# Layer 3: VectorE convolves the four upper rows of image b's strips, TensorE the four lower rows of both halves in joint rounds, and ScalarE copies the halo rows

## The chip, the cores and the metric

The kernel runs on one core of a Trainium2 chip. The metric is the device time of one execution in microseconds; three executions of the kernel before took 14472.04 to 14497.12 us, with a median of 14486.18 us.

## What is computed

A batch of images with 48 channels and 256 x 256 pixels goes through four residual layers, each `x = x + layer(groupnorm(x))`. Layers 1 and 2 are scans along rows and columns. Layer 3, the one that is changed, is cut to this:

```python
y = einsum('oc,bchw->bohw', w_in, x)            # 48 -> 288 channels
f = rfft2(blocks of 8 x 8 of y) * fft_mask      # scaled in the frequency domain
y = irfft2(f)                                   # back to pixels
y = depthwise 3 x 3 convolution of y with w_dw  # zero padding of 1
x1, x2 = split(y, 2, axis=1)                    # 144 channels each
return einsum('oc,bchw->bohw', w_out, gelu(x1) * x2)
```

Layer 0 is built of the same parts (a 1x1 convolution, a depthwise 3 x 3 one, a gated product, an 8 x 8 DFT), in another order and with 96 gated channels.

## The kernel before, in words

Everything is in float32, and a float32 matmul shows as two records in the trace.

`layer3` takes two images, a and b, at a time: two pairs, each cut into 32 strips of RB = 8 rows and a 33rd short step, the tail, which holds the last row of the convolution. That makes 64 full strips and two tails. The convolution's output is one row behind its input, so a strip needs two rows of the strip above it, its halo.

One strip runs through these steps (lines of the profile in brackets):

- `fetch` loads x (SyncE's DMA queue), `normed` applies the group norm on ScalarE and gives the tile `u` (L909).
- `turned` transposes `u` on TensorE into `pt` (L921), and ScalarE copies that to `xt` (L925). `waves` applies the DFT, `pf` (L935), and ScalarE copies it to `xf` (L936).
- `spectrum` multiplies by `w_in` on TensorE, `pz` (L946), and VectorE multiplies the result by the mask into `z` (L948, L952); 16 calls a strip, in eight pieces of two.
- `pixels` turns `z` back into pixels, `pp` (L977), and ScalarE copies them into one of the five tiles `z_a0`, `z_a1`, `z_b0`, `z_b1`, `z_m` (L981). Tile `z_a0` holds the first 128 of the 144 channels of x1 of image a, `z_a1` those of x2; `z_m` holds the remaining 16 channels of both halves and both images. Before that the two halo rows are copied from the tile's own lower end: by ScalarE for `z_m` (L968), by GpSimd for the other four (L970).
- `taps` is the convolution on TensorE (L994): for each of the nine taps, eight matmuls with a diagonal 32 x 32 weight, four pairs of rows by two blocks of 32 channels, summed in the PSUM tile `pd`.
- `gate`: Gelu of x1 on ScalarE, `gl` (L1008), and the product with x2 on VectorE, `g_a`, `g_b` or `g_m` (L1009).
- `mixed` is the product with `w_out` on TensorE, `po` (L1022), 40 matmuls a strip of 32 rows by 64 columns of the array; VectorE adds the residual, `xo` (L1035), and SyncE's queue stores it.

All PSUM tiles come from one pool of four buffers (`ps_w`), each of two banks.

The order of TensorE's work is written by hand (`manual_schedule` for that engine); the other engines' queues are ordered by a scheduler at build time. Two generators `lane(0)` and `lane(1)` give the taps: lane 0 works on channel blocks 0 and 1, lane 1 on blocks 2 and 3, each through a0, a1, gate, b0, b1, gate, and m in every second strip. A third generator, `work`, gives all other pieces. `in_turns` draws them together: in each turn it takes one tap from each lane, a joint round, and then as many pieces as their costs allow, with a credit of `pace` for each lane that moved. Lane 1 starts four rounds later. A piece has a condition, and the pieces come in order: `back` (pixels) waits until both lanes have taken the tile's former strip, `store` (mixed) until all taps of the strip are taken. A lane gates strip n only once strip n - 1 is stored.

Layer 0 has the same machinery with one generator more: `aside` runs "units" on VectorE beside the lanes. A unit convolves a tile with eight `scalar_tensor_tensor` taps for each half of its rows (L313) on an accumulator that ScalarE starts with the first tap (L307). Then follow Gelus on ScalarE (L321, L322). In layer 0 the orders of both TensorE and VectorE are written by hand.

Of the kernel before, what the change touches and what calls it, by code (L numbers as in the profile page):

```python
# [15 lines left out]
C = 48  # L16
# [12 lines left out]
class Net:  # L29
# [782 lines left out]
    def layer3(self, x, scs):  # L812
# [2 lines left out]

        nc, tc, W, H, NQ, HD = self.nc, self.tc, self.W, self.H, self.NQ, HID3
        NM, NR, WP, R2 = 128, HID3 - 128, W + 2, MM // W
        steps = [(p, s) for p in range(self.NP) for s in range(H // RB + 1)]  # L820
        tail = lambda step: step[1] == H // RB
        with ExitStack() as st:
            pool = lambda name, bufs, **k: st.enter_context(tc.tile_pool(name=name, bufs=bufs, **k))
            wp, io, mid = pool("w3", 1), pool("io3", 2), pool("mid3", 1)
            ps_w = pool("ps3w", 4, space=PSUM)
            st.enter_context(tc.manual_schedule(engines={mybir.EngineType.PE}))


            parts = [(0, 0, NM), (HD, NM, NM), (NM, 2 * NM, NR), (HD + NM, 2 * NM + NR, NR)]
# [23 lines left out]
            for k in range(3):  # L853
                for t in range(9):
                    nc.vector.tensor_scalar(diag[:, k, t, :], eye, wd[:, k, t : t + 1], None, ALU.mult)


            wo = wp.tile([128, 6, 64], F32, name="wo")
            nc.gpsimd.memset(wo, 0.0)
            for j in range(4):  # L860
                s = slice(32 * j, 32 * j + 32)
                nc.sync.dma_start(
                    wo[s, 0:4, 0:C], self.a["L3_w_out"][0:NM, :].rearrange("(k c) o -> c k o", c=32)
                )
                for b in range(2):
                    at = 32 * j + NR * b
                    nc.sync.dma_start(wo[at : at + NR, 4 + b, 0:C], self.a["L3_w_out"][NM:HD, :])
# [35 lines left out]

            def normed(step):
                raw, sc = raw_of[step], scp[step[0]]
                u = mid.tile([112, NQ, 2, RB, PW // 2], F32, name="u")
                for e in range(2):
                    for l in range(2):
                        nc.scalar.activation(  # L909
                            u[:, l::2, e].rearrange("p v h w -> p v (h w)"),  # L910
                            raw[0:112, e, :, :, l * 8 : l * 8 + 8].rearrange("p (v f) h w -> p v (f h) w", f=2),
                            AF.Identity, bias=sc[0:112, 1:2], scale=sc[0:112, 0:1],
                        )
                return u
# [13 lines left out]
                return xt  # L928

            def waves(xt):  # L930
                xf = mid.tile([112, NQ, 128], F32, name="xf")
                for q0 in range(0, NQ, 8):
                    pf = ps_w.tile([128, 8, 128], F32, name="pf", tag="w")
                    for q in range(8):
                        nc.tensor.matmul(pf[0:112, q, :], xt[:, q0 + q, :], self.dft_p, start=True, stop=True)  # L935
                    nc.scalar.copy(xf[:, q0 : q0 + 8, :], pf[0:112])  # L936
                return xf
# [23 lines left out]
            def pixels(step, g, k):  # L961

                n, at, old = (64, 64 * (step[1] % 2), 64 - 64 * (step[1] % 2)) if g == "m" else (128, 0, 0)
                t, above = zt[g][at : at + n], zt[g][old : old + n]
                if step[1] == 0:
                    nc.gpsimd.memset(t[:, 0:2, 1 : W + 1], 0.0)
                elif g == "m":
                    nc.scalar.copy(t[:, 0:2, 1 : W + 1], above[:, RB : RB + 2, 1 : W + 1])  # L968
                else:
                    nc.gpsimd.tensor_copy(t[:, 0:2, 1 : W + 1], above[:, RB : RB + 2, 1 : W + 1])  # L970
                if tail(step):
                    nc.gpsimd.memset(t[:, 2, 1 : W + 1], 0.0)
                    return
                for q0 in range(0, NQ, 8):
                    pp = ps_w.tile([128, 2, RB, 4 * PW], F32, name="pp", tag="w")
                    for q in range(8):
                        nc.tensor.matmul(  # L977
                            pp[0:n, q // 4, :, q % 4 * PW : (q % 4 + 1) * PW],
                            z[:, q0 + q, k * NM : k * NM + n], self.idft, start=True, stop=True,
                        )  # L980
                    nc.scalar.copy(  # L981
                        t[:, 2 : RB + 2, 1 + q0 * PW : 1 + (q0 + 8) * PW].rearrange("p h (k w) -> p k h w", k=2),
                        pp[0:n],
                    )
# [3 lines left out]
            def taps(step, g, half, blocks, pd):  # L988
                for t in range(9):
# [8 lines left out]
                            )  # L998
                    yield True

            def gate(step, img, k0, x1, x2):
                n = 32 if tail(step) else 128
                m = W if tail(step) else MM
                flat = lambda ap: ap.rearrange("p k r w -> p k (r w)")[0:n, :, 0:m]
                gl = io.tile([128, 2, MM], F32, name="gl")
                to = gated[img]
                k1 = k0 + (1 if img == "m" else 2)
                nc.scalar.activation(gl[0:n, 0 : k1 - k0, 0:m], flat(x1), AF.Gelu)  # L1008
                nc.vector.tensor_tensor(to[0:n, k0:k1, 0:m], gl[0:n, 0 : k1 - k0, 0:m], flat(x2), ALU.mult)  # L1009

            def mixed(step):

                p, s = step
                h0 = s * RB - 1
                js, n = (range(1), 1) if tail(step) else (range(4), R2)
                pos = [ps_w.tile([128, 2, R2, W], F32, name="po", tag="w") for _ in js[::2]]
                for i in range(5):
                    for j in js:
                        for b in range(2):
                            r = slice(32 * j, 32 * j + 32)  # L1020
                            src = gated["m"][r, 0] if i == 4 else gated["ab"[b]][r, i]
# [29 lines left out]
            def lane(l):  # L1051

                for n, step in enumerate(steps):
                    for img in ("a", "b") + (("m",) if step[1] % 2 == l else ()):
                        pds = []
                        for half in range(1 if img == "m" else 2):
                            g = img if img == "m" else f"{img}{half}"
                            while (step, g) not in ready:
# [8 lines left out]
                        else:  # L1067
                            gate(step, img, 2 * l, *pds)

            def work():  # L1070

                def back(step, k):
# [3 lines left out]
                        pixels(step, order[k], k)  # L1078
                        ready.add((step, order[k]))

                    free = lambda: last not in steps or k == 4 or taken.get((last, order[k]), 0) == 2
                    return free, 0.0 if tail(step) else 3.8, go

                def both(*fs):
                    return lambda: [f() for f in fs]
# [2 lines left out]
                always = lambda: True  # L1088

                def front(step):  # L1090
                    yield always, 1.8, lambda: state.update(xt=turned(state["u"]))
                    yield always, 3.8, lambda: state.update(xf=waves(state["xt"]))

                def spectra():
                    for q in range(0, NQ, 2):
                        yield always, 1.2, both(*[lambda q=q + i: spectrum(state["xf"], q) for i in range(2)])

                def store(step):
                    full = lambda: all(taken.get((step, g), 0) == (1 if g == "m" else 2) for g in order)

                    def go():
                        mixed(step)
                        out.add(step)

                    return full, 4.5, go

                fetch(steps[0])
                state["u"] = normed(steps[0])
# [24 lines left out]
                        yield back(nxt, 1)  # L1133
                yield store(steps[-1])

            self.in_turns([lane(0), lane(1)], work(), 0.6)


@with_exitstack
# [103 lines left out]
```

## Time and profile before

| what | us |
|---|---|
| median of three runs | 14486.18 |
| the profiled execution | 14477.21 |
| its span, first to last instruction | 14475.4 |
| TensorE busy | 13474.0 (93%) |
| VectorE busy | 5981.7 (41%) |
| ScalarE busy | 3295.6 (23%) |
| GpSimd busy | 1496.9 (10%) |
| layer 3, from 9064 us to the end | 5411.4 |

Durations in the profile are those of one execution. "PE" is TensorE, "PEld" its weight loads, "DVE" VectorE, "ACT" ScalarE, "POOL" GpSimd, "SP" SyncE. A group of instructions is shown with its line, engine and operation, then output and inputs with the shape, the count, the busy time in us and the mean of one in ns, and last the engine's idle time before it with what ended that. Matmuls overlap each other, so the mean of one is longer than its share of the time. The chain of waits goes back from the last instruction to what released it each time.

### The profile page before, as it was taken

The page shows a single profiled execution, that of the slowest core. Times are in us where ns is not written, and L with a number is a line of the kernel's source. Part 1 is how long each engine was busy: PE and PEld are TensorE (multiplying, and loading weights), DVE is VectorE, ACT ScalarE, POOL GpSimd, SP SyncE. Part 2 cuts the span into 40 slices and gives each one's busy share as a digit, 9 for nine tenths or more (in the row PEclk, how much of TensorE's full clock was granted, in tenths as well). Part 3 has the DMA queues.
Part 4 walks back from the last instruction along what each step waited for, and adds up shares of the span by engine and source line. Part 5 has one row for each costly group of instructions (what it writes and reads, how often), then busy time and mean ns, then how long its engine had stood idle before and what let it go on. Part 6 is the DMA issues. An engine that isn't in the chain of part 4 may idle for free.

```text
span 14475.4 us, 377862 instructions
## 1 busy us (share of the span) xinstructions
PE 13474.0 (93%) x175216; PEld 8571.1 (59%) x175216; DVE 5981.7 (41%) x10946; ACT 3295.6 (23%) x3108; POOL 1496.9 (10%) x1228
## 2 busy tenths in 40 slices
PE   2999999999998998899989988899999999999999
PEld 1444444446776775667767756566666666666666
DVE  6777777773333344533333445222222222222222
ACT  1333333332232000022320000222222222222222
POOL 0000010000000014400000144000000000000000
PEclk9999999999999998999999988999999999999999
DMA  7222222217756867677577676211111111111110
GB/s 166 53 49 53 54 51 51 54 41 146 145 144 162 152 132 190 160 156 145 145 167 151 135 190 156 31 20 24 21 20 24 20 20 20 24 20 20 24 20 18
DMA packets 1168867, 1221.55 MB, mean 84 GB/s; under 512 B 1025860, under 2 KB 1030460, under 8 KB 1106428
## 3 DMA queue, kind: packets, MB, share of 16 engines
q1 hardware_dynamic: 1069180, 649.60, 23.5%
q0 software_dynamic: 87488, 445.55, 11.0%
q10 hardware_dynamic: 10624, 102.24, 3.5%
q8 instruction: 1375, 22.53, 0.7%
q14 instruction: 200, 1.64, 0.0%
HBM read 699.82 MB, written 497.42 MB: 83 GB/s over the span
## 4 chain that ended last, share of the span: by engine, by line
PE 80%; DVE 8%; DMA 6%; issue 2%; ACT 1%; POOL 1%; SPq 1%; ACTq 0%; DVEq 0%; POOLq 0%
PE acc L598 33%; PE pd L994 20%; PE pp L977 8%; PE pd L278 4%; PE pz L946 4%; DVE acc L313 3%; DMA blk<-x 3%; PE po L1022 2%; PE pf L935 2%; PE ph L249 2%; DMA x<-blk 1%; PE pf L386 1%; DVE xo L419 1%; DMA gx<-in_x 1%; PE py L355 1%
## 5 line engine op out<-in xcount | busy, mean ns | idle before, releaser
L598 PE MATMUL acc<-line,w_down 96*96 96x256 f32 x12240 | 2649.9, 379 | 43.8 <-DMA in<-x 23.3
L598 PEld LDWEIGHTS acc<-line,w_down 96*96 96x96 f32 x12240 | 1995.6, 163 | 697.5 <-issue 44.6
L994 PE MATMUL pd<-z_b,diag 32*32 32x512 f32 x37152 | 1810.9, 596 | 10.5 <-DVE g_a L1009 10.5
L994 PE MATMUL pd<-z_a,diag 32*32 32x512 f32 x37152 | 1794.4, 596 | 0.1
L598 PE MATMUL acc<-line,w_left 96*96 96x256 f32 x6120 | 1360.8, 385 | 246.9 <-DVE line L781 246.9
L598 PE MATMUL acc<-line,w_right 96*96 96x256 f32 x6120 | 1336.9, 381 | 103.0 <-DVE line L742 39.1
L598 PEld LDWEIGHTS acc<-line,w_left 96*96 96x96 f32 x6120 | 1015.9, 166 | 591.5 <-DVE line L781 252.9
L278 PE MATMUL pd<-main,diag 32*32 32x512 f32 x36864 | 1337.7, 601 | 10.5 <-DVE g L292 5.4
L313 DVE SCALAR_TENSOR_TENSOR acc<-rest,wd,acc 128x1024 f32<-128x1024 f32 x1024 | 1313.7, 1324 | 72.5 <-ACT acc L307 70.6
L977 PEld LDWEIGHTS pp<-c_idft,z 128*128 128x128 f32 x10240 | 1156.8, 181 | 287.0 <-issue 265.3
L598 PEld LDWEIGHTS acc<-line,w_right 96*96 96x96 f32 x6120 | 1003.3, 164 | 436.6 <-DVE line L742 40.7
L977 PE MATMUL pp<-c_idft,z 128*128 128x128 f32 x10240 | 1223.8, 278 | 17.6 <-ACT z_b L981 17.6
L994 PEld LDWEIGHTS pd<-z_a,diag 32*32 32x32 f32 x37152 | 697.7, 103 | 508.1 <-issue 318.8
L948 DVE TENSOR_TENSOR z<-pz,mask 128x512 f32<-128x512 f32 x1024 | 701.5, 685 | 698.5 <-PE pz L946 698.5
L278 PEld LDWEIGHTS pd<-main,diag 32*32 32x32 f32 x36864 | 524.3, 103 | 681.6 <-issue 505.4
L994 PEld LDWEIGHTS pd<-z_b,diag 32*32 32x32 f32 x37152 | 619.0, 103 | 455.5 <-issue 278.6
L742 DVE SCALAR_TENSOR_TENSOR line<-acc,b_right,in 96x256 f32<-96x256 f32 x1020 | 489.4, 480 | 882.2 <-PE acc L598 836.8
L661 DVE TENSOR_TENSOR line<-acc,in 96x256 f32<-96x256 f32 x1020 | 429.1, 421 | 928.3 <-PE acc L598 900.2
L701 DVE SCALAR_TENSOR_TENSOR line<-acc,b_down,in 96x256 f32<-96x256 f32 x992 | 476.2, 480 | 808.5 <-PE acc L598 808.5
L791 POOL TENSOR_TENSOR blk<-blk,line 96x1024 f32<-96x1024 f32 x248 | 705.5, 2873 | 861.2 <-DVE line L781 447.4
L102 ACT ACTIVATE nrm<-nrm 96x2 f32<-96x2 f32 (+1 forms) x4 | 0.8, 204 | 3331.1 <-DVE nrm L101 3331.1
L1008 ACT ACTIVATE gl<-pd 128x1024 f32<-128x1024 f32 (+2 forms) x330 | 302.3, 926 | 1970.8 <-PE pd L994 1639.3
(147 smaller groups left out, 12161.3 us busy)
## 6 DMA issues: line engine op xcount, KB each, us to landing
blk<-x ACTq DMA_DIRECT2D x64, 1536.0 KB, 24.0
in<-x SPq DMA_DIRECT2D x248, 384.0 KB, 11.1
dn<-line POOLq DMA_DIRECT2D x124, 768.0 KB, 9.6
rt<-line POOLq DMA_DIRECT2D x124, 768.0 KB, 10.3
in<-rt SPq DMA_DIRECT2D x124, 768.0 KB, 7.3
in<-dn SPq DMA_DIRECT2D x120, 768.0 KB, 7.1
in<-up SPq DMA_DIRECT2D x240, 384.0 KB, 11.1
up<-blk POOLq DMA_DIRECT2D x56, 1536.0 KB, 24.0
```

The lines of the kernel that those rows point to most:

```text
L278: nc.tensor.matmul(pd[32 * j : 32 * j + 32, i], diag[s, t, :], z[s, R2 * j + t // 3 : R2 * j + t // 3 + R2, t % 3 : t % 3 + W], start=(t = ...
L313: nc.vector.scalar_tensor_tensor(to, at(t, r), wd[:, 1, t : t + 1], to, ALU.mult, ALU.add)
L598: self.nc.tensor.matmul(acc, w[:, t, :], carry[:, :, t : t + m], start=(t == 0), stop=(t == 2))
L661: nc.vector.tensor_tensor(blocks(inner(line)), blocks(acc), xin[p][:, :, r % 2, :, r // 2, :], ALU.add)
L701: nc.vector.scalar_tensor_tensor(inner(line), acc, bd, new[p][r], ALU.add, ALU.add)
L742: nc.vector.scalar_tensor_tensor(blocks(inner(line)), blocks(acc), br, new, ALU.add, ALU.add)
L791: (nc.vector if w0 == 0 else nc.gpsimd).tensor_tensor(part, part, inner(ln[p][:, f::2])[..., lo:hi].rearrange("p w i h -> p i h w"), ALU.add)
L946: nc.tensor.matmul(pz[:, b, 0 : 2 * HD], xf[s, q, :], wi[s, :], start=True, stop=True)
L948: nc.vector.tensor_tensor(z[:, q, 0 : 2 * n].rearrange("p (b c) -> p b c", b=2), pz[:, :, 0:n], mask[:, :, 0:n].to_broadcast([128, 2, n]), ...
L977: nc.tensor.matmul(pp[0:n, q // 4, :, q % 4 * PW : (q % 4 + 1) * PW], z[:, q0 + q, k * NM : k * NM + n], self.idft, start=True, stop=True,)
L994: nc.tensor.matmul(pd[32 * j : 32 * j + 32, i, 0:n, :], diag[s, 2 if g == "m" else half, t, :], zt[g][s, R2 * j + t // 3 : R2 * j + t // 3 ...
L1008: nc.scalar.activation(gl[0:n, 0 : k1 - k0, 0:m], flat(x1), AF.Gelu)
```

## The change

All of it is in `layer3`.

- Image b's taps are divided. The four upper rows of a strip's output (row pairs 0 and 1) are convolved on VectorE by `unit`, which `aside` runs: for each half, b0 and b1, ScalarE starts the accumulator with tap 0, VectorE adds taps 1 to 8 over 128 channels by 4 rows by 256 columns. After half 0 ScalarE applies Gelu to it, after half 1 VectorE multiplies the two.
- The four lower rows stay on TensorE in `lower_taps`: in one round a lane takes both halves (x1 to output partitions 0 to 63, x2 to 64 to 127), so image b takes nine rounds of a lane where it took 18. `lower_gate` follows.
- `mixed` takes the upper rows of image b from the accumulator with two matmuls of full depth and a new weight tile `wo_b`, ahead of the others, and leaves out the eight pairs that did this (b = 1, j < 2, i < 4).
- The halo rows of a and b are copied by ScalarE instead of GpSimd.
- VectorE's order in layer 3 is written by hand too. `store` waits for the unit's product as well, `back` for the unit's taps, and the pieces have new costs; `pace` is 0.65 instead of 0.6.
- `u` and `xf` share one buffer.

The diff, cut to its core:

```diff
-            st.enter_context(tc.manual_schedule(engines={mybir.EngineType.PE}))
+            st.enter_context(tc.manual_schedule(engines={mybir.EngineType.PE, mybir.EngineType.DVE}))
+            HR = RB // 2
...
+            wo_b = wp.tile([128, 64], F32, name="wo_b")
+            nc.gpsimd.memset(wo_b, 0.0)
+            nc.sync.dma_start(wo_b[:, 0:C], self.a["L3_w_out"][0:NM, :])
...
-                u = mid.tile([112, NQ, 2, RB, PW // 2], F32, name="u")
+                u = mid.tile([112, NQ, 2, RB, PW // 2], F32, name="u", tag="u")
...
-                xf = mid.tile([112, NQ, 128], F32, name="xf")
+                xf = mid.tile([112, NQ, 128], F32, name="xf", tag="u")
...
-                elif g == "m":
+                else:
                     nc.scalar.copy(t[:, 0:2, 1 : W + 1], above[:, RB : RB + 2, 1 : W + 1])
-                else:
-                    nc.gpsimd.tensor_copy(t[:, 0:2, 1 : W + 1], above[:, RB : RB + 2, 1 : W + 1])
...
+            def lower_taps(step, blocks, pd):
+                for t in range(9):
+                    for half in range(2):
+                        for j in range(2, 4):
+                            to = slice(64 * half + 32 * (j - 2), 64 * half + 32 * (j - 1))
+                            for i, k in enumerate(blocks):
+                                s = slice(32 * k, 32 * k + 32)
+                                nc.tensor.matmul(
+                                    pd[to, i], diag[s, half, t, :],
+                                    zt[f"b{half}"][s, R2 * j + t // 3 : R2 * j + t // 3 + R2, t % 3 : t % 3 + W],
+                                    start=(t == 0), stop=(t == 8),
+                                )
+                    yield True
+
+            def lower_gate(k0, pd):
+                gl = io.tile([128, 2, MM], F32, name="gl")
+                flat = pd.rearrange("p k r w -> p k (r w)")
+                nc.scalar.activation(gl[64:128], flat[0:64], AF.Gelu)
+                nc.vector.tensor_tensor(gated["b"][64:128, k0 : k0 + 2], gl[64:128], flat[64:128], ALU.mult)
...
+            whole, full = {}, set()
+
+            def unit(step, half):
+                g, rows, made = f"b{half}", 1 if tail(step) else HR, []
+                at = lambda t: zt[g][:, t // 3 : t // 3 + rows, t % 3 : t % 3 + W]
+
+                def start():
+                    acc = mid.tile([128, HR, W], F32, name=f"acc{half}", tag=f"acc{half}", bufs=2 - half)
+                    made.append(acc[:, 0:rows])
+                    nc.scalar.activation(made[0], at(0), AF.Identity, bias=none, scale=wd[:, half, 0:1])
+
+                def tap(t):
+                    nc.vector.scalar_tensor_tensor(
+                        made[0], at(t), wd[:, half, t : t + 1], made[0], ALU.mult, ALU.add
+                    )
+                    if t == 8:
+                        taken[step, g] = taken.get((step, g), 0) + 1
+
+                def curve():
+                    nc.scalar.activation(made[0], made[0], AF.Gelu)
+                    whole[step] = made[0]
+
+                def product():
+                    nc.vector.tensor_tensor(whole[step], whole[step], made[0], ALU.mult)
+                    full.add(step)
+
+                taps = [(0.05 + 0.31 * rows, lambda t=t: tap(t)) for t in range(1, 9)]
+                last = [(3, 0.0, curve)] if half == 0 else [(2, 1.28, product)]
+                return lambda: (step, g) in ready, start, taps, last
...
+                part = whole.pop(step)
+                for j in js[:2]:
+                    nc.tensor.matmul(
+                        pos[0][64:128, j, 0:n, :], wo_b, part[:, R2 * j : R2 * j + n, :], start=True, stop=False
+                    )
                 for i in range(5):
                     for j in js:
                         for b in range(2):
+                            if b and j < 2 and i < 4:
+                                continue
...
+                        if img == "b":
+                            while (step, "b0") not in ready or (step, "b1") not in ready:
+                                yield False
+                            if not tail(step):
+                                pds.append(ps_w.tile([128, 2, R2, W], F32, name="pd", tag="w"))
+                                yield from lower_taps(step, (2 * l, 2 * l + 1), pds[0])
+                            for g in ("b0", "b1"):
+                                taken[step, g] = taken.get((step, g), 0) + 1
+                            while n and steps[n - 1] not in out:
+                                yield False
+                            if pds:
+                                lower_gate(2 * l, pds[0])
+                            continue
...
-                        yield always, 1.2, both(*[lambda q=q + i: spectrum(state["xf"], q) for i in range(2)])
+                        yield always, 1.2, both(*[lambda q=q + i: spectrum(state["xf"], q) for i in range(2)]), 2.0
...
-                    return full, 4.5, go
+                    return done, 6.4, go, 3.5
...
-            self.in_turns([lane(0), lane(1)], work(), 0.6)
+            side = self.aside([unit(s, k) for s in steps for k in range(2)])
+            self.in_turns([lane(0), lane(1)], work(), 0.65, side)
```

More of the change, by code (lines that the diff above doesn't have):

```diff
@@ L855, in layer3 @@
                     nc.vector.tensor_scalar(diag[:, k, t, :], eye, wd[:, k, t : t + 1], None, ALU.mult)
+            none = wp.tile([128, 1], F32, name="none")
+            nc.gpsimd.memset(none, 0.0)
             wo = wp.tile([128, 6, 64], F32, name="wo")
             nc.gpsimd.memset(wo, 0.0)
+            wo_b = wp.tile([128, 64], F32, name="wo_b")
+            nc.gpsimd.memset(wo_b, 0.0)
+            nc.sync.dma_start(wo_b[:, 0:C], self.a["L3_w_out"][0:NM, :])
             for j in range(4):
@@ L1068, in lane @@
                             gate(step, img, 2 * l, *pds)
+            units = {g: 3 if g[0] == "b" else 1 if g == "m" else 2 for g in order}
             def work():
@@ L1079, in go @@
                         ready.add((step, order[k]))
-                    free = lambda: last not in steps or k == 4 or taken.get((last, order[k]), 0) == 2
-                    return free, 0.0 if tail(step) else 3.8, go
+                    free = lambda: last not in steps or k == 4 or taken.get((last, order[k]), 0) == units[order[k]]
+                    return free, 0.0 if tail(step) else 3.8, go, 0.0
                 def both(*fs):
@@ L1090, in front @@
                 def front(step):
-                    yield always, 1.8, lambda: state.update(xt=turned(state["u"]))
-                    yield always, 3.8, lambda: state.update(xf=waves(state["xt"]))
+                    yield always, 1.8, lambda: state.update(xt=turned(state["u"])), 0.0
+                    yield always, 3.8, lambda: state.update(xf=waves(state["xt"])), 0.0
                 def spectra():
                     for q in range(0, NQ, 2):
-                        yield always, 1.2, both(*[lambda q=q + i: spectrum(state["xf"], q) for i in range(2)])
+                        yield always, 1.2, both(*[lambda q=q + i: spectrum(state["xf"], q) for i in range(2)]), 2.0
                 def store(step):
-                    full = lambda: all(taken.get((step, g), 0) == (1 if g == "m" else 2) for g in order)
+                    done = lambda: step in full and all(taken.get((step, g), 0) == units[g] for g in order)
                     def go():
```

## The prediction

> **What bounds the kernel now.** I read the busy time by stretches first, for the last layer alone and for two of its strips; then the chain of waits, for the length of a strip.
>
> ```profile
> 9064.00:14475.40 5411.40, 5348.13 (x106162) 3309.34 (x106162) 1329.24 (x2918) 1414.89 (x1547) 174.28 (x294) 1.00 0.12 21
> 12037.98:12205.00 167.02, 165.39 (x3307) 102.40 (x3312) 41.15 (x90) 43.87 (x48) 4.93 (x8) 1.00 0.12 21
> ...
> 11870.95 17.94 PE pd L994 x503
> 12037.98 17.94 PE pd L994 x503
> ```
>
> Columns of the first two: stretch and length, then busy us (instructions) of TensorE, its weight loads, VectorE, ScalarE, GpSimd, then granted clock, DMA share, GB/s. Layer 3 takes 5411 us, TensorE is busy 99% of it at full clock, VectorE 25%, ScalarE 26%. The same place of the chain comes back after 167.03 us, two strips: **83.5 us a strip**, 64 full strips.
>
> Then the groups of layer 3 and (last two) layer 0, and TensorE's waits:
>
> ```profile
> L994 PE MATMUL pd<-z_b,diag 32*32 32x512 f32 x37152 | 1810.9, 596 | 10.5 <-DVE g_a L1009 10.5
> L968 ACT COPY z_m<-z_m 64x512 f32<-64x512 f32 x64 | 39.5, 617 | 2.0
> L925 ACT COPY xt<-pt 128x896 f32<-128x896 f32 x128 | 109.9, 909 | 195.4 <-PE pt L921 195.4
> L307 ACT ACTIVATE acc<-rest,none,wd 128x1024 f32<-128x1024 f32 x122 | 151.6, 1242 | 188.9 <-DVE rest L261 187.2
> L313 DVE SCALAR_TENSOR_TENSOR acc<-rest,wd,acc 128x1024 f32<-128x1024 f32 x985 | 1264.3, 1324 | 72.5 <-ACT acc L307 70.6
> ...
> PE pp L977 <- ACT z_b L981: 17.6, 15, 1.2
> PE pd L994 <- DVE g_a L1009: 10.5, 46, 0.2
> ```
>
> Here TensorE waits for nobody: 28 us in 64 strips. So each microsecond of waiting that the change brings is lost in full, as each microsecond of work it takes away is won.
>
> Layer 0 already splits its convolution between TensorE and VectorE, so its timeline shows what such a split can cost:
>
> ```profile
> 1533.57 1.06 ACT L321 ACTIVATE gr<-acc 64x1024 f32<-64x1024 f32 x1 [0.46 <-DVE acc L313]
> 1534.77 1.06 ACT L322 ACTIVATE gr<-acc 64x1024 f32<-64x1024 f32 x1
> 1535.85 1.04 ACT L323 COPY acc<-acc 64x1024 f32<-64x1024 f32 x1
> 1536.80 1.01 ACT L289 ACTIVATE gl<-pd 128x1024 f32<-128x1024 f32 x1
> 1537.86 1.75 PE L372 MATMUL pt<-c_ident,y 112*128 112x112 f32 x16 [1.58 <-ACT gl L289]
> ```
>
> TensorE stands 1.58 us because the Gelu that frees its PSUM buffer (L289) is queued on ScalarE behind Gelus that waited for VectorE's taps.
>
> [...] a joint round of both lanes (32 records of 0.596 us) comes every 1.06 us. [...]
>
> **The change, part by part** (per full strip).
>
> *Taps leave TensorE.* Counted in both instruction orders, joint rounds fall from 2664 to 2052, 9 a full strip and 36 short ones in the two tails. 9 x 1.06 = **9.5 us less**.
>
> *The output product.* 32 of its 80 records on image b go, 4 of full depth come (2 matmuls, two records each) ahead of the rest. Image a still needs the ten groups that set the 4.47 us of the old product. The four cost 1.98 us in layer 0 (L257, 112 deep, 512 columns, four in 1.98). They use only half the columns, so the last may overlap: bounds 0 and 2.0; I take **1.8 more**.
>
> *VectorE.* 16 taps of 128x1024 and one product. Layer 0's tap takes 1.324 us, but one follows the other every 1.20, since its neighbours work on two halves of a tile. Here each tap reads what the one before wrote. Bounds 1.20 and 1.37 (duration and a handoff); I take 1.32. 16 x 1.32 + 1.2 = 22 us on an engine with 62 us free: its amount costs nothing, its order may.
>
> *ScalarE.* Two starts (1.24), one Gelu (1.06), four halo copies (0.62) taken over from GpSimd, where they waited up to 27 us for taps without harm: 6 us on an engine with 61 free. The wo_b load and the memsets are once: nothing beside the 20 us that the first matmul waits for a weight load anyway; 2 us if not.
>
> *The new waits.* VectorE's queue is now in program order, ScalarE's is the scheduler's. In the changed kernel's order ScalarE has, after each store: Gelu of acc0 (waits for VectorE's 8th tap), Gelu of a0 (frees a PSUM buffer), two pixel copies of z_b1, start of acc1, halo copy of z_b1 (waits for the 5th tap of acc1), then the copies of xt that the next DFT needs. VectorE has the eight xo additions, the acc0 taps left over, and all of acc1. Behind a tap thus queue a PSUM release and a transpose copy that TensorE needs. One strip, from the end of the output product:
>
> VectorE: xo 2.8 (eight took 2.74), 5 taps to 9.4. ScalarE: Gelu 10.5, Gelu of a0 11.5. TensorE: 4 rounds and pp (3.77) done at 8.1, then needs the buffer: **waits 3.4**. ScalarE: two copies (1.03) to 13.5, start to 14.8. VectorE: 5 taps to 21.4. ScalarE: halo 22.0, xt 22.9. TensorE: from 11.5 three rounds, pt (1.7), one round: 17.5, then needs xt: **waits 5.4**. Small waits in the spectra (a pz buffer used again after 0 or 2 matmuls, where VectorE's 0.74 is in between) and for g_m: 0.9. Sum 9.7.
>
> The other three patterns, walked the same way: pair 0 with 4 taps left 4.0 + 4.6 + 1.7 = 10.3; pair 1 with 6 left 5.0 + 4.1 + 1.0 = 10.1; pair 1 with 4 left: product for g_m 3.0, b's taps for a g_a multiply that stands behind 4 taps of acc1 5.4, one pp on a single buffer 1.2, spectra on a single buffer 4.7, together 14.3. Mean **11.1 us more**.
>
> *Sum:* -9.5 + 1.8 + 11.1 = +3.4 us a strip, x 64 = +215. Tails: 36 short rounds gone, one chain of 16 short taps bare at the very end: 10 us either way, taken as 0. The profiled execution took 14477 us (span 14475), 9 under the median; against the median 14486 + 215 = **14700**.
>
> With a tap at 1.20 the walk gives 9.7 of waits, +2.0 a strip, 14615; with 1.37, +4.1, 14750. An error of 1 us in the walk's other terms is 64 us: own range 14550 to 14850.
>
> **Rivals.** *The cover holds* (faster): VectorE and ScalarE run early enough, TensorE waits little. For it: layer 0 has the same design, busier (VectorE 2160 of 2900 us), and its TensorE idles only 220 us in 64 strips, 3.4 each. With 3.4 here: -9.5 + 1.8 + 3.4 = -4.3 x 64: **14210**. Against it: layer 0's tail taps are spread through the strip, here 12 to 14 stand in one block between store and DFT. Place: the waits for pd's release and for xt. It decides below 7.7 us of waits a strip: then faster. *They cancel* (7 to 8 us): **14486**. *The waits are larger*: taps over 1.4 us, or a halo copy that also holds up the pixel copies of image a; at 15 us of waits a strip, +7.3 x 64: **14950**. That VectorE doesn't take over the rows is excluded by the order, which has its 16 taps a strip.
>
> **How the numbers follow.** Forecast 0.70, cover holds 0.15, cancel 0.07, larger 0.08. Within 0.2% (29 us) is about what a measurement of this kernel can tell from no change. Faster by more 0.15, same 0.07, slower 0.78. The range goes from 14470 (takes in most of the cancel case) to 14850 and leaves out 0.15 below and 0.05 above.
>
> **What would show it.** Right: in layer 3 a strip takes 86 to 88 us, TensorE's busy share falls to some 87%, VectorE's rises to 50%; TensorE's longest waits are pf for ScalarE's xt (4 to 6 us, 48 times) and pd or pp for ScalarE's gl (3 to 5 us), ScalarE's are the Gelu of acc0 and the z_b1 halo copy for VectorE's taps; the dependent taps come every 1.32 us. Wrong: a strip under 83 us, or waits on ScalarE under 1 us; then ScalarE's order or the tap's pace was misjudged. If the four full-depth records take over 2.5 us, that term was.

## The result and the profile after

The changed kernel takes **14831.6 us** (median of four executions, 14821.3 to 14836.3) against 14484.2 for the kernel before: ratio 1.0239, 95% interval 1.0221 to 1.0256. The forecast was 14700. Its profiled execution has a span of 14819.5 us, 344.1 more than before. Of e10's four executions below, two took 15497 and 25725 us at a mean granted clock of 0.88 and 0.51, where the other two had 0.97, and are left out.

The busy time by stretches of the changed kernel comes first: all of layer 3, then six stretches of one strip of pair 0 that follow each other. The columns are those of the prediction's first view; the last three are the granted clock (the share of its full clock that TensorE was given), DMA share and GB/s.

```profile
9064.00:14819.50 5755.50, 5178.42 (x86662) 3005.19 (x86662) 2734.59 (x4036) 1775.43 (x1997) 15.73 (x30) 0.95 0.10 20
10020.01:10023.42 3.41, 1.02 (x22) 0.83 (x29) 1.26 (x1) 2.12 (x3) 0.00 (x0) 1.00 0.36 35
10023.42:10026.83 3.41, 3.41 (x65) 1.29 (x66) 0.41 (x1) 3.38 (x4) 0.00 (x0) 0.50 0.02 5
10026.83:10030.25 3.42, 3.42 (x80) 2.28 (x79) 3.35 (x3) 0.07 (x1) 0.00 (x0) 1.00 0.00 0
10030.25:10033.66 3.41, 0.84 (x32) 0.00 (x0) 3.30 (x4) 0.58 (x2) 0.00 (x0) 1.00 0.02 5
10033.66:10037.07 3.41, 2.51 (x12) 2.51 (x13) 3.30 (x4) 2.58 (x4) 0.00 (x0) 0.50 0.00 0
10037.07:10040.49 3.42, 3.42 (x18) 3.42 (x18) 1.14 (x1) 1.01 (x1) 0.00 (x0) 0.50 0.00 0
```

The whole 344 us lie in layer 3 (5755.5 against 5411.4). TensorE is busy 90% of it and idle 577 us, where it was idle 63. But its busy time fell by 170 us only, 2.7 a strip, where the prediction took 7.7 away. The granted clock tells why: it was 1.00 throughout layer 3 before, and is 0.95 now. It isn't 0.95 evenly. TensorE stands still from 10020.94 to 10023.33 and from 10031.09 to 10034.56, and after each of these waits it works at **half the clock** (0.50) for some microseconds.

The clock records of the traces show when. In layer 3 every change of the clock lies on a grid of 3.413 us, the stretches of the view above (all 225 changes from 9110 us on in the changed kernel, to 5 ns). In the changed kernel half clock lasts one stretch of the grid 67 times out of 113, two 40 times and three 4 times. Ahead of a fall stands a stretch in which TensorE was little busy: 1.02 and 0.84 of 3.41 us ahead of the two falls here. Counted over the twelve traces of this case, from 9110 us on, all 430 stretches at full clock in which TensorE was busy less than 0.40 of the time were followed by half clock, 152 of 326 from 0.40 to 0.62, and 2 of 17309 above that; in the changed kernel alone it was 90 of 90, 22 of 55 and 1 of 2932. Full clock never came back after a stretch that was busy less than 0.80; in the changed kernel the 112 stretches ahead of a return were busy at least 0.83.

The timeline of the same strip, ScalarE, VectorE and TensorE:

```profile
10017.40 0.62 ACT L975 COPY z_b<-z_b 128x512 f32<-128x512 f32 x1 [12.25 <-DVE acc L1053]
10021.31 1.06 ACT L1060 ACTIVATE acc<-acc 128x1024 f32<-128x1024 f32 x1 [3.29 <-DVE acc L1053]
10022.27 1.01 ACT L1035 ACTIVATE gl<-pd 128x1024 f32<-128x1024 f32 x1
10025.15 1.24 ACT L1050 ACTIVATE acc<-z_b,none,wd 128x1024 f32<-128x1024 f32 x1
10033.08 0.62 ACT L975 COPY z_b<-z_b 128x512 f32<-128x512 f32 x1 [6.18 <-DVE acc L1053]
10033.61 1.71 ACT L932 COPY xt<-pt 128x896 f32<-128x896 f32 x2
...
10014.71 6.56 DVE L1053 SCALAR_TENSOR_TENSOR acc<-z_b,wd,acc 128x1024 f32<-128x1024 f32 x5
10026.42 10.53 DVE L1053 SCALAR_TENSOR_TENSOR acc<-z_b,wd,acc 128x1024 f32<-128x1024 f32 x8 [5.15 <-ACT acc L1050]
...
10017.10 3.84 PE L982 MATMUL pp<-c_idft,z 128*128 128x128 f32 x32
10023.33 5.01 PE L999 MATMUL pd<-z_a,diag 32*32 32x512 f32 x96 [2.39 <-ACT gl L1035]
10028.26 1.75 PE L928 MATMUL pt<-c_ident,u 112*128 112x112 f32 x16
10034.56 6.63 PE L942 MATMUL pf<-c_dft_p,xt 128*112 128x128 f32 x32 [3.47 <-ACT xt L932]
10041.11 3.41 PE L999 MATMUL pd<-z_a,diag 32*32 32x512 f32 x96
```

The chain is the one that the prediction forecast: VectorE's last acc0 tap ends at 10021.3, the Gelu of acc0 has waited for it (L1060), the Gelu of a0 that frees TensorE's buffer stands behind that. Then the halo copy of z_b1 (L975) waits 6.18 us for the fifth tap of acc1, and the copies of xt stand behind that. What was not forecast are two durations on TensorE. The 96 records (three joint rounds) after the first wait take 5.01 us, at full clock 3.41 (last line); pf takes 6.63 us, at full clock 3.75. Taps come every 1.31 us (10.53 for eight).

TensorE's longest waits in the changed kernel, and the two of ScalarE that cause them (total us, times, longest):

```profile
PE pf L942 <- ACT xt L932: 139.7, 42, 5.1
PE pd L999 <- ACT gl L1035: 104.1, 31, 8.1
PE pd L1015 <- DVE g_a L1036: 64.3, 15, 4.4
PE pp L982 <- ACT gl L1035: 54.9, 17, 6.2
PE po L1079 <- DVE g_m L1036: 48.5, 16, 4.7
PE pz L953 <- DVE z L959: 44.3, 57, 1.0
...
ACT z_b L975 <- DVE acc L1053: 1036.5, 127, 14.7
...
ACT acc L1060 <- DVE acc L1053: 221.4, 64, 15.5
```

Before, TensorE's waits within the strips were the 28 us of the prediction's view. Groups by form, for taps on TensorE and on VectorE and for pf:

```profile
L999 PE MATMUL pd<-z_a,diag 32*32 32x512 f32 x36864 | 1749.1, 623 | 119.2 <-ACT gl L1035 104.1 <-ACT xt L932 6.4 <-ACT z_b L986 5.8
L1053 DVE SCALAR_TENSOR_TENSOR acc<-z_b,wd,acc 128x1024 f32<-128x1024 f32 x1024 | 1315.4, 1285 | 856.0 <-ACT acc L1050 826.8
L942 PE MATMUL pf<-c_dft_p,xt 128*112 128x128 f32 x2048 | 329.6, 337 | 139.7 <-ACT xt L932 139.7
```

A tap record on TensorE has a mean of 623 ns where it had 596, one of pf 337 where a record at full clock takes 272: the half clock spread over all strips. Over stretches of 0.5 us of layer 3 I summed TensorE's busy time multiplied by the clock that was missing: 240 us, 3.7 a strip; the same sum is under 3 us in the kernel before.

The two pairs differ. From pf to pf a strip takes on average 87.0 us in pair 0 and 90.5 in pair 1; before it was 82.9 and 83.5 (the prediction's 83.5 is from pair 1). From strip 4 to 30 of a pair, the 87.0 us are 7.2 of idle time, 3.5 lost to half clock and 76.3 of other work, the 90.5 are 9.6, 4.0 and 76.9. In e2 to e6 below the last term stays at 76.2 to 76.7, so idle time and half clock account for all but 0.5 us of their differences.

### The profile page after: what moved, and what is told of

Read it like the earlier page. It is cut to its first block, busy times and chain, and to the rows that moved or that the text cites. A ratio compares the mean times of both kernels' runs of the same rounds, so it can differ in the third digit from the quotient of the medians.

```text
span 14819.5 us, 338365 instructions
## 1 busy us (share of the span) xinstructions
PE 13306.5 (90%) x155716; PEld 8266.5 (56%) x155716; DVE 7384.4 (50%) x12064; ACT 3658.1 (25%) x3558; POOL 1339.3 (9%) x974
## 4 chain that ended last, share of the span: by engine, by line
PE 69%; DVE 16%; DMA 6%; ACT 4%; issue 2%; POOL 1%; SPq 1%; ACTq 0%; DVEq 0%; POOLq 0%
PE acc L598 32%; PE pp L982 7%; DVE acc L1053 6%; PE pd L999 6%; PE pd L1015 4%; PE pz L953 4%; PE pd L278 4%; DVE acc L313 3%; DMA blk<-x 3%; PE pf L942 2%; PE po L1089 2%; PE ph L249 2%; DMA x<-blk 2%; PE pf L386 1%; DVE xo L419 1%
## 5 line engine op out<-in xcount | busy, mean ns | idle before, releaser
L1053 DVE SCALAR_TENSOR_TENSOR acc<-z_b,wd,acc 128x1024 f32<-128x1024 f32 (+1 forms) x1056 | 1330.8, 1260 | 857.3 <-ACT acc L1050 826.8
L1015 PE MATMUL pd<-z_b,diag 32*32 32x512 f32 x18432 | 1010.1, 605 | 86.7 <-DVE g_a L1036 64.3
L999 PEld LDWEIGHTS pd<-z_a,diag 32*32 32x32 f32 x37152 | 627.6, 104 | 694.5 <-issue 378.4
L953 PE MATMUL pz<-wi,xf 48*128 48x288 f32 x4096 | 683.4, 443 | 68.7 <-DVE z L959 44.3
## 6 DMA issues: line engine op xcount, KB each, us to landing
in<-x SPq DMA_DIRECT2D x248, 384.0 KB, 11.1
```

Of the source, the lines that this page charges most:

```text
L953: nc.tensor.matmul(pz[:, b, 0 : 2 * HD], xf[s, q, :], wi[s, :], start=True, stop=True)
L999: nc.tensor.matmul(pd[32 * j : 32 * j + 32, i, 0:n, :], diag[s, 2 if g == "m" else half, t, :], zt[g][s, R2 * j + t // 3 : R2 * j + t // 3 ...
L1015: nc.tensor.matmul(pd[to, i], diag[s, half, t, :], zt[f"b{half}"][s, R2 * j + t // 3 : R2 * j + t // 3 + R2, t % 3 : t % 3 + W], start=(t ...
L1053: nc.vector.scalar_tensor_tensor(made[0], at(t), wd[:, half, t : t + 1], made[0], ALU.mult, ALU.add)
```

## The experiments

Each kernel is compared with the kernel before on the same chip; that one's medians were 14487.6 (e1 to e4), 14489.2 (e5 to e8) and 14494.5 us (e9, e10).

### e1_no_units: TensorE's part of the change without VectorE's

```diff
+            blank = wp.tile([128, HR, W], F32, name="blank")
+            nc.gpsimd.memset(blank, 0.0)
+            for s in steps:
+                full.add(s)
+                whole[s] = blank
+                for g in ("b0", "b1"):
+                    taken[s, g] = 1
-            side = self.aside([unit(s, k) for s in steps for k in range(2)])
-            self.in_turns([lane(0), lane(1)], work(), 0.65, side)
+            self.in_turns([lane(0), lane(1)], work(), 0.65)
```

> This kernel leaves out VectorE's part of the convolution: no starts, taps, Gelus and products of the units, and the upper rows of image b are taken from a tile of zeros; all else is the changed kernel. Theory A (the loss is waits of TensorE for ScalarE and VectorE, 8.0 us a strip, and the half clock that follows them, some 3.7 us a strip; the work itself got shorter): without the units both go, a strip takes 83.5 - 9.5 + 2.7 = 76.7 us, the kernel 14486 - 6.8 x 64 = 14050 us (14000 to 14110), the granted clock in layer 3 is 1.00 and TensorE is busy 98%. Rival B (TensorE's work itself became slower, by the joint rounds, the full-depth product and the halo copies on ScalarE): the time stays at 14700 or more with the clock at 0.95.

Measured 14131.8 us, ratio 0.9757 (0.9742 to 0.9771). By stretches, all of layer 3 and five strips of pair 0, then four strips of pair 0 of the kernel before:

```profile
9064.00:14124.30 5060.30, 4908.57 (x86662) 2865.62 (x86662) 1333.75 (x2914) 1571.64 (x1799) 17.59 (x41) 0.99 0.12 22
9909.70:10289.00 379.30, 377.17 (x6765) 221.70 (x6757) 103.17 (x225) 122.42 (x140) 0.00 (x0) 1.00 0.12 23
...
9890.52:10221.97 331.45, 331.00 (x6604) 203.17 (x6593) 82.47 (x180) 88.19 (x97) 9.86 (x16) 1.00 0.13 22
```

In pair 0 a strip takes 379.3 / 5 = 75.9 us at full clock, **7.0 less than before (82.9); the prediction's terms for TensorE's own work, -9.5 + 1.8, say 7.7**. Rival B is out: the number of TensorE's records is that of the changed kernel (86662), and without the units it needs 270 us less for them. Pair 1 takes 80.3 us even here, which is why the time lies above the expected range: 4.4 us a strip have nothing to do with VectorE's taps, which e1 leaves out (e5 shows what they come from).

### e2_halo_gpsimd, e3_gelu_late, e4_both: ScalarE's queue

e2 takes the halo copies of a and b back to GpSimd, e3 moves the Gelu of acc0 behind the copies of xf (it is issued four taps later, and `keep_in_program_order` pins it behind all that ScalarE was given before), e4 does both.

```diff
-                else:
+                elif g == "m":
                     nc.scalar.copy(t[:, 0:2, 1 : W + 1], above[:, RB : RB + 2, 1 : W + 1])
+                else:
+                    nc.gpsimd.tensor_copy(t[:, 0:2, 1 : W + 1], above[:, RB : RB + 2, 1 : W + 1])
```

```diff
-                    nc.scalar.activation(made[0], made[0], AF.Gelu)
+                    tc.keep_in_program_order(nc.scalar.activation(made[0], made[0], AF.Gelu))
-                last = [(3, 0.0, curve)] if half == 0 else [(2, 1.28, product)]
+                last = [(7, 0.0, curve)] if half == 0 else [(2, 1.28, product)]
```

> The changed kernel with the halo copies of images a and b back on GpSimd. Theory A (ScalarE's strict queue: the z_b1 halo copy waits for VectorE's fifth tap and holds the xt copies up): the wait of pf for xt (3.5 to 4.4 us in pair 0, up to 2.4 in every second strip of pair 1) goes, and with it the half clock in pf (2.9 us); the wait for gl behind the Gelu of acc0 stays. About 6.5 x 31 + 1.2 x 32 = 240 us less: 14590 us (14530 to 14660). Rival C ([...] the copies come so late that the pixel copies wait for them): taps get longer than 1.31 us or new waits on GpSimd appear, 14750 to 14900 us.

> The changed kernel with the Gelu of acc0 pinned in ScalarE's queue behind the xf copies instead of ahead of the Gelu of a0; its halo copies stay on ScalarE. Theory A: the wait for gl (2.4 to 2.8 us in pair 0) and its half clock (1.6 us) go, the start of acc1 comes some 4 us earlier, so VectorE's taps of acc1 and the halo copy behind them end earlier too and the pf wait shrinks to 0 to 1 us: 9 to 11 us a strip in pair 0, 3 in pair 1: 14830 - 310 - 100 = 14420 us (14350 to 14560). Rival D (the halo copies alone are what holds ScalarE up; the Gelu just takes the waiting over): less than 80 us won, 14750 us or more.

> Both edits: halo copies of a and b on GpSimd and the Gelu of acc0 late. Theory A: nothing stands behind a tap on ScalarE any more; in pair 0 TensorE waits under 1 us a strip at a clock near 1.00 (77 to 78 us a strip); in pair 1 the waits on VectorE's own queue stay (g_m before the output product 3, g_a before the lower taps 4, spectra 2 us a pair of strips, with some half clock), some 82 us a strip: 14486 - 6 x 32 - 1.5 x 32 = 14250 us (14170 to 14400), faster than the kernel before. Rival D: VectorE's queue, not ScalarE's, sets the end in both pairs: 14600 us or more.

| kernel | us | ratio to before | strip in pair 0, pair 1 |
|---|---|---|---|
| changed | 14831.6 | 1.0239 (1.0221 to 1.0256) | 87.0, 90.5 |
| e2, halos on GpSimd | 14623.5 | 1.0095 (1.0080 to 1.0110) | 81.0, 90.4 |
| e3, Gelu late | 14660.2 | 1.0120 (1.0105 to 1.0135) | 83.6, 88.8 |
| e4, both | 14344.4 | 0.9902 (0.9886 to 0.9919) | 76.9, 85.3 |

e2 came as expected: the wait for xt is gone from the list, and 6.0 us a strip of pair 0 with it (3.5 to 4.4 of waiting, the rest half clock). e3 won less than I had expected, and the waits of e3 show where it went:

```profile
PE pf L942 <- ACT xt L932: 165.7, 40, 4.4
PE po L1079 <- DVE g_m L1036: 42.6, 14, 4.7
```

The wait for gl is nearly gone, but TensorE then comes to pf earlier, and the copies of xt still stand behind the halo copy of z_b1, which is free 8 us after the start of acc1. In every second strip of pair 0 TensorE waited for gl behind pp: from the end of pp to the first copy of xt it was 12.7 us and is 9.6 now. In the others it waited ahead of pp: those 2.8 us are gone, and from pp to xt it is 9.6 as before. That is most of the 3.4 us that a strip won. I had let the start come earlier without moving TensorE up as well. With both edits nothing is queued behind a tap on ScalarE: e4 has no wait for gl or xt over 1.6 us left, the clock in pair 0 is 1.00, and it is 1% faster than the kernel before:

```profile
9600.00:11500.00 1900.00, 1885.81 (x33342) 1099.36 (x33323) 1063.75 (x1541) 628.57 (x664) 112.71 (x100) 1.00 0.12 23
```

The same VectorE work is in it. So it was the places in ScalarE's queue that cost, not VectorE's 22 us.

### e5_turns and e6_both_turns: why pair 1 is slower

```diff
-                n, at, old = (64, 64 * (step[1] % 2), 64 - 64 * (step[1] % 2)) if g == "m" else (128, 0, 0)
+                n, at, old = (64, 64 * (sum(step) % 2), 64 - 64 * (sum(step) % 2)) if g == "m" else (128, 0, 0)
...
-                    for img in ("a", "b") + (("m",) if step[1] % 2 == l else ()):
+                    for img in ("a", "b") + (("m",) if sum(step) % 2 == l else ()):
```

e5 is this edit on the changed kernel, e6 on e4.

> The changed kernel, where the lane that takes image m alternates through both pairs, by pair plus strip, not by strip alone (with 33 steps a pair, one lane takes m twice in a row at the change of pairs, and the lanes stand otherwise to each other from there on). Theory E (pair 1 is slower only because of this other pattern: there TensorE waits for g_m, g_a and the spectra, even without the units): pair 1 runs like pair 0, 87.0 instead of 90.5 us a strip, 14830 - 3.5 x 32 = 14720 us (14690 to 14760). Rival F (pair 1 is slower for its data or its loads): no change, 14830.

> Halo copies on GpSimd, the Gelu of acc0 late, and the lanes alternating through both pairs. Theory E: pair 1 takes the 76.9 us a strip that pair 0 took with the first two edits, instead of 85.3: 14344 - 8.4 x 32 = 14075 us (14040 to 14140), at a clock of 1.00 in layer 3. Rival F: 14344, no change to the run with the two edits.

e5: 14731.7 us, ratio 1.0167 (1.0151 to 1.0182), 87.0 us a strip in pair 0 and 87.1 in pair 1. e6: **14075.9 us, ratio 0.9711 (0.9695 to 0.9728)**, 76.9 and 77.0 us. Both are within 12 us of what was expected; rival F is out. Pair 1's own waits (for g_m, g_a and the spectra) came from how the two lanes stand to each other after one lane took m twice in a row. Layer 3 of e6, and its two longest waits of TensorE:

```profile
9064.00:14073.00 5009.00, 4919.66 (x86666) 2886.27 (x86666) 2767.72 (x4051) 1642.27 (x1742) 312.23 (x296) 0.99 0.12 23
...
PE pd L1017 <- DVE z L959: 15.9, 30, 0.5
PE pz L953 <- DVE z L959: 13.8, 26, 0.5
```

VectorE has the work of the changed kernel (55% of layer 3), ScalarE all of it but the halo copies (33%). TensorE waits half a microsecond at a time, up to 1.1 in a few single waits, once the layer has started; the clock is back at 1.00 from 9110 us on.

### e9_b1_alone: which halo copy

```diff
-                elif g == "m":
+                elif g != "b1":
                     nc.scalar.copy(t[:, 0:2, 1 : W + 1], above[:, RB : RB + 2, 1 : W + 1])
```

> As the run with all three edits (e6_both_turns), but of the halo copies only that of z_b1 is on GpSimd; those of a0, a1 and b0 stay on ScalarE, as the change has them. Theory A (the copy of z_b1 alone matters: it queues between the start of acc1 and the copies of xt and waits for VectorE's fifth tap): no difference to the 14076 us of all three edits, 14050 to 14105. Rival J (the copy of z_b0, which also waits for a tap, or the 1.9 us more that ScalarE has to copy hold TensorE up again): waits for gl come back, 14150 us or more.

14085.7 us, ratio 0.9716 (0.9702 to 0.9731), 76.8 us a strip in both pairs: no difference to e6. Of the four halo copies that the change moved, only that of z_b1 does harm, with e6's other two edits in place.

### e8_graded and e7_warm: the half clock

e8 is the kernel before, with no taps of layer 3 on VectorE; only ScalarE's first copy of xt is repeated, which makes TensorE wait.

```diff
-                    nc.scalar.copy(
-                        xt[:, q0 : q0 + 8, :].rearrange("p (k q) c -> p k (q c)", k=2), pt[:, :, 0 : 4 * 112]
-                    )
+                    for _ in range(times if q0 == 0 else 1):
+                        nc.scalar.copy(
+                            xt[:, q0 : q0 + 8, :].rearrange("p (k q) c -> p k (q c)", k=2), pt[:, :, 0 : 4 * 112]
+                        )
...
-                    yield always, 1.8, lambda: state.update(xt=turned(state["u"]))
+                    yield always, 1.8, lambda: state.update(xt=turned(state["u"], 1 + step[1] % 8))
```

> The kernel before (no units, TensorE at full clock throughout) with ScalarE's first copy of xt repeated: strip s makes it 1 + s mod 8 times, so that pf waits for xt by steps of some 0.85 us, from none to some 5 us; nothing else is changed. Theory G: waits of up to some 1.5 us cost themselves alone; from about 2.3 us on pf (3.75 us at full clock) takes 5 to 6.7 us at a granted clock of 0.5. Sum of the waits some 16 us in eight strips, of the half clock some 10: 26 x 8 = 210 us more, 14695 us (14620 to 14760). Rival H (VectorE's taps bring the half clock): waits alone, 14486 + 128 = 14615, and the clock stays 1.00 in layer 3.

14876.0 us, ratio 1.0265 (1.0249 to 1.0280). pf in three strips that follow each other, and all of layer 3:

```profile
10581.86 3.75 PE L936 MATMUL pf<-c_dft_p,xt 128*112 128x128 f32 x32 [0.78 <-ACT xt L926]
...
10667.33 5.41 PE L936 MATMUL pf<-c_dft_p,xt 128*112 128x128 f32 x32 [2.28 <-ACT xt L926]
...
10755.61 5.42 PE L936 MATMUL pf<-c_dft_p,xt 128*112 128x128 f32 x32 [3.91 <-ACT xt L926]
...
9064.00:14875.00 5811.00, 5452.67 (x106164) 3409.85 (x106164) 1331.11 (x2927) 1603.39 (x1772) 173.51 (x294) 0.97 0.12 20
```

The waits became longer than I had meant (up to 8.8 us, because the group norm's copies were queued between the repeats), so the time is above the expected one; the comparison within the kernel is what counts. After 0.8 us pf took 3.75 us in all seven strips; after 2.3 us it took 5.4 in seven of eight, 3.75 in one; from 3.8 us on it took 5.1 to 6.8 in every strip. The one exception fits the grid: its 2.3 us lay across two stretches, 0.8 in one and 1.4 in the next, so neither was less than 0.40 busy; in the other seven one stretch was busy only 0.33 to 0.35. TensorE has the instructions of the kernel before and 105 us more busy time (5452.7 against 5348.1). No VectorE tap is there: rival H is out, the half clock follows the waiting.

e7 was meant to keep TensorE warm in the changed kernel: 12 more matmuls in the wait for xt.

```diff
                     pf = ps_w.tile([128, 8, 128], F32, name="pf", tag="w")
+                    for _ in range(warm if q0 == 0 else 0):
+                        nc.tensor.matmul(pf[0:112, 0, :], self.idft[:, 0:112], self.dft_p, start=True, stop=True)
```

> The changed kernel with 12 matmuls more a strip (128 x 112 by 128 columns, into pf, overwritten by the real ones) in the place where TensorE waits for xt, in pair 0 from strip 7 on; they need 12 x 0.234 = 2.8 us of a wait of 3.3 to 5.0 us. Theory G (the half clock follows from TensorE's idling): what is left of the wait is 0.5 to 2.2 us, pf takes 3.8 us instead of 5.2 to 6.7 in most strips, and although TensorE does more, 1 to 2.5 us a strip are won in 26 strips: 14770 to 14805 us, clock in pair 0 0.97 to 0.98 instead of 0.95. Rival H (the half clock comes from what runs at that moment on other engines, VectorE's taps): pf still takes 5.2 to 6.7 us, the time is 14830 or more.

It took 14910.1 us, ratio 1.0289 (1.0273 to 1.0304), far above the 14770 to 14805 of theory G and where rival H had it. But it decides nothing between G and H, since the added matmuls waited too:

```profile
10054.50 4.54 PE L942 MATMUL pf<-c_dft_p,c_idft 128*112 128x128 f32 x24 [3.55 <-ACT xt L932]
10058.88 3.66 PE L944 MATMUL pf<-c_dft_p,xt 128*112 128x128 f32 x32
```

They need no xt, but they stood the same 3.55 us; that pf's buffer is one that the copy of xt frees would explain it, which no run tests. It does show that the half clock is a stretch of time and not a property of pf: the added records, which come first, took 4.54 us instead of 2.8, and pf behind them has its full speed (3.66 us).

### e10_product: the price of the full-depth product

```diff
+                for j in js[:2]:
+                    nc.tensor.matmul(
+                        pos[0][64:128, j, 0:n, :], wo_b, blank[:, R2 * j : R2 * j + n, :], start=True, stop=False
+                    )
...
-                                start=(i == 0), stop=(i == 4),
+                                start=(i == 0 and not (b and j < 2)), stop=(i == 4),
```

> The kernel before with the two full-depth matmuls (four records, a tile of zeros by weights of zeros) put ahead of its output product; nothing else is changed, so their price stands alone. Theory K (they add their own 1.86 us and hold up the first of the small matmuls behind them, as the product of the changed kernel took 7.27 us against 4.54): 2.7 us a strip, 14486 + 173 = 14660 us (14640 to 14680), at full clock. Rival L (only the term of the prediction, 1.8 us): 14600 us; rival M (they overlap with the small ones): 14500 to 14560.

The two executions that count took 14598.6 and 14615.3 us, too few for an interval; the profile is of the first. Against 14494.5 that is 1.6 to 1.9 us a strip: rival L, the prediction's term.

```profile
10065.08 1.93 PE L1022 MATMUL po<-blank,wo_b 128*64 128x512 f32 x4
10066.94 0.64 PE L1030 MATMUL po<-g_a,wo 32*64 32x512 f32 x1
```

The four records come 1.86 us ahead of the first small one and hold nothing up. The product of the changed kernel takes 0.9 us more for another reason. There the timeline shows VectorE, then a weight load of the product:

```profile
10006.20 1.28 DVE L1053 SCALAR_TENSOR_TENSOR acc<-z_b,wd,acc 128x1024 f32<-128x1024 f32 x1
10007.51 0.69 DVE L1036 TENSOR_TENSOR g_m<-gl,pd 128x512 f32<-128x512 f32 x1
10008.25 0.13 PEld L1089 LDWEIGHTS po<-g_a,wo 32*64 32x64 f32 x1 [0.70 <-DVE g_m L1036]
```

The second po tile takes over the PSUM buffer of m, which the multiply for g_m frees, and that is queued behind taps of acc0. The pause counts as busy, since earlier records are still running. It is a wait on VectorE's queue of 0.9 us a strip, left in e6 too, where the product takes 7.4 us in pair 0 and 6.4 in e1: that is what lies between e6's 76.9 and e1's 75.9.

## Why the prediction was right, and where its size was off

Per strip, the prediction's terms beside what was measured:

| term | forecast | measured | from |
|---|---|---|---|
| TensorE's rounds and product | -9.5 + 1.8 = -7.7 | -7.0 | e1, pair 0 |
| waits that the profile shows | 11.1 with the next line | 8.0 | idle time, 577 - 63 over 64 strips |
| wait for g_m inside the product | in the line above | 0.9 | timeline |
| half clock after waits | 0 | 3.7 | clock by stretches |
| sum | +3.4 | +5.6 | layer 3 itself: 344 / 64 = +5.4 |

- **TensorE's work** was right to 0.7 us, its product to 0.1: 1.86 us against 1.8 (e10). Some 0.3 of the 0.7 are small pauses: TensorE is idle 0.1 us a strip in the view of before under e1 and 0.4 in that of e1. Where the rest is no run shows.
- **VectorE's pace** was right: a dependent tap every 1.31 us, 1.32 taken. Its amount costs next to nothing: e6 has it all and takes 76.9 us a strip, e1 has none of it and takes 75.9. ScalarE's amount is as harmless.
- **The order of the waits** was right, place by place. Where five acc0 taps are left, as in the strip shown, the walk has 3.4 us for the release of pd and 5.4 for xt. The timeline has 2.4 and 3.5, but TensorE had already lost 0.9 in the product ahead of the first wait, and 1.6 by half clock between the two: 3.3 and 5.1. VectorE and ScalarE did what the walk said, to a third of a microsecond.
- **The step that failed** is the sum itself, that a wait costs its own length: TensorE's work behind a wait was put in at the durations of a kernel that never waits. Of the half clock in this strip the 1.6 us before the second wait only filled that wait; the 2.9 us in pf, and in pair 1 those after the waits for g_m and g_a, come on top, as no wait follows that they could fill. The clock records of this case show a clock of 0.50 for whole stretches of 3.413 us. TensorE need not stand idle through a whole stretch for it: a busy share under 0.40 was enough each time (430 of 430), so waits of 2.3 us that fell into one stretch brought half clock (seven of eight in e8, the wait for gl in the changed kernel), while one of 0.8 never did (none of seven in e8).
- **Luck.** The waits came out 2.2 us a strip under the forecast (8.0 + 0.9 against 11.1), in part because slow work filled them. That hid more than half of the 3.7 us that were left out: how close 14700 came is partly luck.
- **Pair 1** was to take 83.5 - 7.7 + 12.2 = 88.0 us and takes 90.5. e5 shows that 3.4 us of it come from how the lanes stand to each other. The walk saw these waits, 12.2 us a strip, and 9.6 are measured; the 4.0 us of half clock behind them are again what it lacks.
- **The rivals.** "The cover holds" was wrong for this kernel, but not far: e4, with the halo copies and one Gelu taken from their places in ScalarE's queue, is 1% faster than before. The reason given against it, 12 to 14 taps in one block, holds only while something that TensorE needs stands behind them. "They cancel" and 14950 didn't come.

The measured terms add up to 0.2 us a strip more than layer 3 shows; the pauses of e1 are in two of them.

## What to carry to other kernels

When work moves to an idle engine, ask for each instruction of the engines beside it what stands behind it in the queue: a Gelu of 1.1 us and halo copies of 0.6 us, of which only that of z_b1 counted in e9, made the difference between 1.0% faster (e4) and 2.4% slower. A wait of TensorE must be priced with what follows it: in these traces, where it left TensorE busy under 0.40 of a stretch of 3.41 us, at least one such stretch ran at half clock (430 of 430) and lost up to 1.7 us of work, often two and 3.4 us (40 of 113 in the changed kernel), unless another wait came right behind. And where a pattern of turns shifts at some point of a loop, each phase needs its own walk and its own measurement.

## What the hardware showed beyond that

A GpSimd copy beside VectorE's taps was slower. In e6 the same copy of 128 x 512 takes 1.64 us for z_b0 or z_b1, while a tap runs (all 128 of them), and 0.62 for z_a, when none does. Nine copies of z_a that did meet a tap took 1.2 to 1.6 us, so it isn't the tile:

```profile
10150.91 1.64 POOL L977 COPY z_b<-z_b 128x512 f32<-128x512 f32 x1 [51.37 <-DVE acc L1055]
10156.84 0.62 POOL L977 COPY z_a<-z_a 128x512 f32<-128x512 f32 x1 [4.29 <-PE pd L1001]
```

Why, the traces don't show. VectorE pays too: the four taps with the first of these copies beside them took 5.46 us, where four at 1.31 us take some 5.25. The copy was off every chain here, so this cost nothing.
